# Moving one VectorE addition two units later in the q and k products of an attention kernel

## The chip, the cores and the metric

The kernel runs on one core of one Trainium2 chip. The core has a matrix engine (TensorE, PE in the profile, whose weight loads have a row of their own, PEld), a vector engine (VectorE, DVE), an activation engine (ScalarE, ACT), GpSimd (POOL) and a sync engine that issues DMAs (SyncE, SP). Matmul results land in PSUM[...], and VectorE and ScalarE read them from there.

The metric is the device time of one execution in microseconds (us). The kernel before takes 2177.04 us, the median of three runs from 2176.34 to 2177.31. A difference of less than about 0.2%, some 4.4 us, can't be told from no change.

## What is computed

The input is 8 images of 512 channels and 32 x 32 positions in float32, so each is a 512 x 1024 matrix. Two layers follow each other:

```python
# layer 0: attention with 8 heads of 64 channels
q = conv1x1(x, Wq, bq);  k = conv1x1(x, Wk, bk);  v = conv1x1(x, Wv, bv)
attn = softmax(einsum('bhdn,bhdm->bhnm', q, k) * scale)
x = x + conv1x1(einsum('bhnm,bhdm->bhdn', attn, v), Wp, bp)
# layer 1: a non-local block without softmax, then a batch norm
f = einsum('bcn,bdn->bcd', theta(x), phi(x)) / n
z = conv1x1(einsum('bcd,bdn->bcn', f, g(x)), W_w, W_b) + x
out = (z - mean(z)) * rsqrt(var(z) + eps) * gamma + beta
```

The change concerns `q` and `k` alone. Each is a product of a 512 x 512 weight and a 512 x 1024 image, plus a bias for each channel.

## The kernel before, in words

**Order of the stages.** The loop at the end of `unshifted` goes through the images. For image b it runs the attention, then q of image b+1, v of image b+1, k of image b+1, then the projection (`pp`) of image b with Wp, then theta and phi (`ptp`), and then the non-local block. TensorE's instructions have a fixed order (`pe` keeps them in program order), so these stages lie behind each other on TensorE.

**A product by seven.** The large products are done in the manner of Winograd's variant of Strassen's scheme, by `seven`: weight and data are cut into quarters 11, 12, 21 and 22, and seven products of quarters, or of sums of quarters, are added to the four quarters of the result. `SEVEN` (line 220) lists for each product its name, the weight and the data that it takes, the PSUM slot and the quarters that read the slot. A slot[...] holds one quarter product of 256 x 512. Some products are added up in the slot itself and read again in between.

**q and k.** From the second image on, three of the seven quarter products are cut in the same way once more (`nested`, line 240): 3 times 7 inner products of 128 x 256, each with an add into q or k on VectorE, or a first write on ScalarE. The other four are full quarter products (`FOUR`, line 234): product 0 is W11 x11, product 1 is s1t1, product 2 is s2t2, product 3 is s3t3. Products 0, 2 and 3 add up in slot 0, and product 1 alone lies in slot 1. The full products are spread over 16 units (`HALVES`), each unit being one 128 x 128 x 512 matmul of the code; float32 shows each of them as two rows in the trace. Product 1 is done by units 4, 5, 10 and 11. After each unit come so many inner products as `STEPS` says: two after each of units 5 to 12, one after units 13, 14 and 15. The inner products are counted here from 0 to 20; 14 and 15 follow unit 11, 16 and 17 follow unit 12, 18 follows unit 13, 19 unit 14 and 20 unit 15.

**Inner products wait for adds.** In one inner round, products 0, 2, 4 and 6 share a place in PSUM, and 1 and 3 share another. So inner product 16 can't start before VectorE has added inner product 14 to q or k, 17 waits for the add of 15, 18 for that of 16, and 20 for that of 18.

**Reading the slots.** `READS` (lines 237 and 238) says after which unit a slot of the full products is read, and for which quarter. A read marked `True` is the first for its quarter and is done by ScalarE as two activations of 128 x 512 with the bias (line 386). One marked `False` is an add on VectorE of 128 x 1024 (line 319). Within a unit these reads stand ahead of the unit's inner products, except in unit 15.

**Order on VectorE.** In q the adds have a fixed order (`pin` is `dve`, which keeps them in program order). In k they have none of their own: a planner that lays out the instructions of each engine in advance may put them elsewhere. VectorE also makes differences of image data in these stages (`more_sums`, line 201, and `inner_parts`, line 213): the dictionary `fills` puts them behind a unit, in k after units 5, 7, 11, 12, 13 and 14.

**PSUM tags.** When a stage ends, its slots go to the next. Slot 0 of the stage that follows (v after q, `pp` after k) is slot 1 of q or k.

Of the kernel before, what the change touches and what calls it, by code (L numbers as in the profile page):

```python
# [22 lines left out]
def attention_nonlocal_kernel(tc: tile.TileContext, a: dict, out: bass.AP):  # L23

    sound = unshifted(tc, a, out)
    with tc.If(sound < P):
        shifted(tc, a, out)
# [3 lines left out]
def unshifted(ctx: ExitStack, tc: tile.TileContext, a: dict, out: bass.AP):  # L31
# [184 lines left out]
    def quarters_of(t):  # L216
# [17 lines left out]
    FOUR = tuple((*one[:4], ()) for one in (SEVEN[0], SEVEN[1], SEVEN[2], FIVE[4]))  # L234
    HALVES = ((0, 0), (0, 1), (1, 0), (2, 0), (2, 1), (1, 1), (3, 0), (3, 1))
    STEPS = {2: [0] * 4 + [1] * 14, 3: [0, 0, 0, 1, 1, 2, 2, 2, 2, 2, 2, 2, 2, 1, 1, 1]}
    READS = {3: ((0, "11", True),), 9: ((0, "12", True),), 11: ((1, "22", True), (1, "12", False)),
             15: ((0, "22", False), (0, "21", False))}

    def nested(name, stage, w, data, tags, first, add):  # L240
# [17 lines left out]
    def seven(name, w, data, positions_out, first, add, between=None, early=False,  # L258
# [14 lines left out]
        def read(reads, ps):  # L273
            for to, is_first in reads:
                (first if is_first else add)(to, ps)

        products = FOUR if three else FIVE if inner else EARLY if early else SEVEN
        for n, m in HALVES if three else ((n, None) for n in range(len(products))):
# [15 lines left out]
            for to_ps, at, lhsT, rhs, k in work:  # L294
# [3 lines left out]
                for ahead in (True, False):  # L298
                    for one, to, is_first in READS.get(unit, ()) if three and ahead == (unit < 15) else ():
                        read(((to, is_first),), slots[one])  # L300
# [818 lines left out]
```

## Time and profile before

| what | value | how to read it |
|---|---|---|
| time | 2177.04 us | median of three runs |
| span of the profiled run | 2174.1 us | first to last instruction |
| TensorE busy | 2129.2 us (98%) | matmuls are pipelined, so this is not TensorE at its peak |
| VectorE busy | 1399.6 us (64%) | an average over stages of very different load |
| ScalarE busy | 746.5 us (34%) | |
| granted TensorE clock | 0.996 | nearly full speed throughout |
| DMA | 106 GB/s mean | |
| `q<-q,pq_in_s`, 128 x 256 | 119 x 419 ns | adds of inner products on VectorE |
| `q<-q,pq`, 128 x 1024 | 25 x 1216 ns | adds of full products on VectorE |
| `q<-pq,bq`, 128 x 512 | 48 x 684 ns | first writes on ScalarE |

In a timeline each row gives start and duration in us, engine, line, operation, output and inputs, the shape, how often it came in a row, and in brackets how long the engine had been idle before it and what released it. In a list of waits the columns are the total in us, how often, and the longest.

### The profile page before, as it was taken

The numbers are of one execution on the slowest core, as the hardware profiler recorded it, in microseconds if no ns is written. First come the engines' busy times: TensorE is split into PE (matmuls) and PEld (weight loads), VectorE is DVE, ScalarE is ACT, GpSimd is POOL, SyncE is SP. The second block draws the span as 40 slices with busy tenths as digits, with TensorE's granted clock in tenths as the row PEclk, the third lists the DMA queues.
The fourth block names the chain that finished last, engine by engine and source line by source line (L and its number), as shares of the span: only waits on it lengthen the run. The fifth ranks groups of instructions, "written<-read, shape, count | busy, mean of one in ns | idle before, by whom it ended". The sixth has DMA issues, their size and how long they took to land.

```text
span 2174.1 us, 30056 instructions
## 1 busy us (share of the span) xinstructions
PE 2129.2 (98%) x12510; PEld 1120.5 (52%) x12510; DVE 1399.6 (64%) x1690; ACT 746.5 (34%) x854; POOL 205.1 (9%) x256
## 2 busy tenths in 40 slices
PE   9999999999999999999999999999999999999996
PEld 4534664356733567335663366633666337643462
DVE  6466756666576665766657666576674675757736
ACT  1464104631046310463105621056212652056206
POOL 0111100110001100011000100011000110011000
PEclk9999999999999999999999999999999999999998
DMA  6333443334143331433324342233434235122658
GB/s 219 136 49 61 136 154 124 49 69 128 72 129 50 77 115 72 132 50 77 111 87 119 49 94 92 105 105 49 106 122 166 40 47 137 51 56 39 216 204 337
DMA packets 53375, 229.97 MB, mean 106 GB/s; under 512 B 9712, under 2 KB 16112, under 8 KB 45680
## 3 DMA queue, kind: packets, MB, share of 16 engines
q1 hardware_dynamic: 41552, 198.21, 27.0%
q0 software_dynamic: 10192, 28.46, 10.9%
q8 instruction: 100, 1.64, 0.3%
q10 hardware_dynamic: 1488, 1.32, 0.2%
q14 instruction: 43, 0.35, 0.0%
HBM read 140.79 MB, written 46.27 MB: 86 GB/s over the span
## 4 chain that ended last, share of the span: by engine, by line
PE 94%; ACT 2%; DVE 2%; DMA 1%; issue 0%; ACTq 0%; DVEq 0%
PE ps L456 20%; PE po L482 20%; PE pv L295 9%; PE ptp L295 9%; PE pp L295 7%; PE pk L295 5%; PE pq L295 5%; PE pg L295 4%; PE pq_in_s L250 3%; PE pk_in_s L250 3%; PE pf L622 3%; PE pz L295 2%; PE pp_in_s L250 2%; PE pwf L657 1%; ACT z L773 1%; DVE k L319 1%
## 5 line engine op out<-in xcount | busy, mean ns | idle before, releaser
L459 ACT ACTIVATE e<-ps 128x1024 f32<-128x1024 f32 x512 | 522.9, 1025 | 433.5 <-PE ps L456 428.0
L465 DVE TENSOR_TENSOR acc<-acc,e 128x1024 f32<-128x1024 f32 x384 | 470.0, 1224 | 144.6 <-ACT e L459 141.3
L482 PE MATMUL po<-e,v 64*64 64x512 f32 x4096 | 528.7, 589 | 0.7 <-ACT w_WgT L624 0.7
L456 PE MATMUL ps<-q,k 64*64 64x512 f32 x4096 | 529.1, 589 | 0.0
L482 PEld LDWEIGHTS po<-e,v 64*64 64x64 f32 x4096 | 156.5, 133 | 283.4 <-issue 275.7
L456 PEld LDWEIGHTS ps<-q,k 64*64 64x64 f32 x4096 | 155.6, 133 | 284.1 <-issue 275.0
L495 POOL DMA_DIRECT2D fold<-acc x189 | 147.2, 779 | 984.9 <-DMA fold<-acc 583.4
L463 DVE TENSOR_TENSOR acc<-e,e 128x1024 f32<-128x1024 f32 x64 | 78.3, 1224 | 143.7 <-ACT e L459 143.7
L645 ACT ACTIVATE g<-pg,gb 128x512 f32<-128x512 f32 x31 | 21.3, 687 | 418.9 <-PE pg L295 418.8
L295 PE MATMUL pv<-w_WvT,t_x 128*128 128x256 f32 x512 | 116.4, 381 | 0.0
L295 PE MATMUL ptp<-w_tp,t_x 128*128 128x256 f32 x512 | 114.4, 379 | 0.0
L411 ACT COPY v<-pv 128x1024 f32<-128x1024 f32 x32 | 32.4, 1012 | 224.6 <-PE pv L295 224.6
L295 PEld LDWEIGHTS pv<-w_WvT,t_x 128*128 128x128 f32 x512 | 96.6, 190 | 18.5 <-issue 5.7
L295 PEld LDWEIGHTS ptp<-w_tp,t_x 128*128 128x128 f32 x512 | 97.3, 190 | 13.2
L423 POOL TENSOR_SCALAR q<-q,gates 128x1024 f32<-128x1024 f32 x32 | 35.3, 1114 | 700.3 <-DVE gates L421 700.3
L295 PE MATMUL pp<-t_o,w_WpT 128*128 128x512 f32 x208 | 100.8, 592 | 0.0
L295 PE MATMUL pq<-t_x,w_WqT 128*128 128x512 f32 x200 | 99.9, 593 | 0.4 <-DVE w_WqT L784 0.4
L295 PE MATMUL pk<-t_x,w_WkT 128*128 128x512 f32 x200 | 100.0, 592 | 0.0
L295 PE MATMUL ptp<-w_tp,x 128*128 128x256 f32 x384 | 87.4, 381 | 0.0
L295 PE MATMUL pv<-w_WvT,x 128*128 128x256 f32 x384 | 86.8, 379 | 0.0
L319 DVE TENSOR_TENSOR q<-q,pq_in_s 128x256 f32<-128x256 f32 x119 | 48.3, 419 | 49.1 <-PE pq_in_s L250 46.0
L295 PEld LDWEIGHTS ptp<-w_tp,x 128*128 128x128 f32 x384 | 72.4, 190 | 13.0 <-issue 3.6
(179 smaller groups left out, 2282.9 us busy)
## 6 DMA issues: line engine op xcount, KB each, us to landing
fold<-acc POOLq DMA_DIRECT2D x189, 128.0 KB, 3.1
w_WqT<-kept_WqT SPq DMA_DIRECT2D x7, 2368.0 KB, 8.9
w_WkT<-kept_WkT SPq DMA_DIRECT2D x7, 2368.0 KB, 9.0
r<-den_d SPq DMA_DIRECT2D x32, 512.0 KB, 7.1
x<-in_x_dram SPq DMA_DIRECT2D x31, 512.0 KB, 6.0
w_WpT<-kept_WpT SPq DMA_DIRECT2D x6, 2176.0 KB, 8.6
w_WvT<-kept_WvT SPq DMA_DIRECT2D x7, 1792.0 KB, 7.1
w_tp<-kept_tp SPq DMA_DIRECT2D x7, 1792.0 KB, 7.3
```

The lines of the kernel that those rows point to most:

```text
L250: pe(nc.tensor.matmul(ps, a[wi], d[di], start=s not in begun, stop=True, skip_group_check=True))
L295: pe(nc.tensor.matmul(to_ps, lhsT(k), rhs(k), start=(s, at) not in begun, stop=(k == nk - 1), skip_group_check=True))
L319: pin(nc.vector.tensor_tensor(at, at, ps if len(ps.shape) == 3 else ps.unsqueeze(1), ALU.add))
L411: seven(f"pv_{b}", w, data, True, lambda q, ps: nc.scalar.copy(at(q), as_v(ps)), lambda q, ps: dve(nc.vector.tensor_tensor(at(q), at(q), a ...
L423: nc.gpsimd.tensor_scalar(q[:, p, :], q[:, p, :], gate[:, p:p + 1], 1.0, ALU.mult, ALU.mult)
L456: pe(nc.tensor.matmul(ps[c * P // 2:(c + 1) * P // 2, j, :], k[r, p, keys], q[r, p, h * 512:(h + 1) * 512], start=True, stop=True, skip_gr ...
L459: nc.scalar.activation(e, ps, AF.Exp, scale=SCALE)
L463: nc.vector.tensor_tensor(accs[u], es[u, 0], e, ALU.add)
L465: ins = nc.vector.tensor_tensor(accs[u], accs[u], e, ALU.add)
L482: pe(nc.tensor.matmul(ps[j * D:(j + 1) * D, r, :], v[keys, m, (2 * p + j) * D:(2 * p + j + 1) * D], e[keys, j, :], start=(m == 0), stop=(m ...
L495: nc.gpsimd.dma_start(to, part_of, accum_op=ALU.add)
L622: pe(nc.tensor.matmul(ps[:, c, :], tp[:, i, c * P:(c + 1) * P], tp[:, i, CI:], start=(i == 0), stop=(i == NB - 1)))
```

## The change

The addition of product 1 (slot 1) to quarter 12 moves from unit 11 to unit 13. At unit 11 there stays only ScalarE's first write of quarter 22 from the same slot. The instruction itself is the same, and no other is added or removed. It is meant to keep VectorE free for the adds of the inner products while ScalarE reads slot 1, so that the addition stands in VectorE's queue where the slot is free to be read.

```diff
-    READS = {3: ((0, "11", True),), 9: ((0, "12", True),), 11: ((1, "22", True), (1, "12", False)),
+    READS = {3: ((0, "11", True),), 9: ((0, "12", True),), 11: ((1, "22", True),), 13: ((1, "12", False),),
              15: ((0, "22", False), (0, "21", False))}
```

`READS` is used by the stages with three inner rounds only: q and k of images 1 to 7, 14 stages in all.

## The prediction

> **What bounds the kernel now.** I read the page first, then TensorE's waits, then the timeline of one q stage and one k stage. The share of the chain that ended last says whose time counts:
>
> ```profile
> PE 94%; ACT 2%; DVE 2%; DMA 1%; issue 0%; ACTq 0%; DVEq 0%
> ```
>
> TensorE carries the span, so only time taken from TensorE's row counts. The little that isn't PE in this chain is where the change can act. TensorE's waits, longest first, show where:
>
> ```profile
> PE pk_in_s L250 <- DVE k L319: 10.1, 8, 1.4
> PE pq_in_s L250 <- DVE q L319: 9.9, 7, 1.4
> PE warm_ps L339 <- DVE heads L325: 1.1, 1, 1.1
> ```
>
> Of all idle time of TensorE, 20.0 us lies in the q and k stages, and it is one wait of 1.42 us in each of the 14 (plus one of 0.23 in the first k). Every one sits in the same place. The timeline of the q stage of image 2, PE's weight loads left out:
>
> ```profile
> 474.36 1.02 PE L295 MATMUL pq<-t_x,w_WqT 128*128 128x512 f32 x2
> 475.22 0.59 PE L250 MATMUL pq_in_s<-x,w_WqT 128*128 128x256 f32 x2
> 475.42 1.27 ACT L386 ACTIVATE q<-pq,bq 128x512 f32<-128x512 f32 x2 [0.38 <-PE pq L295]
> 475.65 0.59 PE L250 MATMUL pq_in_s<-i_x,w_WqT 128*128 128x256 f32 x2
> 476.08 1.02 PE L295 MATMUL pq<-t_x,w_WqT 128*128 128x512 f32 x2
> 476.72 1.22 DVE L319 TENSOR_TENSOR q<-q,pq 128x1024 f32<-128x1024 f32 x1 [2.17 <-ACT q L386]
> ...
> 478.04 0.75 DVE L319 TENSOR_TENSOR q<-q,pq_in_s 128x256 f32<-128x256 f32 x2
> ...
> 478.52 0.70 PE L250 MATMUL pq_in_s<-i_x,w_WqT 128*128 128x256 f32 x2 [1.42 <-DVE q L319]
> 479.06 0.59 PE L250 MATMUL pq_in_s<-x,w_WqT 128*128 128x256 f32 x2
> ```
>
> The first row is unit 11. ScalarE reads slot 1 for quarter 22 from 475.42 to 476.69. The add to quarter 12 reads the same slot: VectorE stands idle for 2.17 us, released by that ScalarE read, and starts at 476.72. Behind it in VectorE's queue are the adds of inner products 14 and 15 (478.04, the second 0.33 later). Inner product 16 waits for the first and begins at 478.52.
>
> How much is lost? I take the cadence rather than the 1.42 us, since matmul ends are modelled. A unit takes 0.86 us (474.36 to 475.22), an inner product 0.43 (475.22 to 475.65). With unit 12 at 476.08, product 16 is due at 476.94, product 17 at 477.37 and unit 13 at 477.80. In the trace unit 13 comes at 479.49: **1.69 us lost** a q stage. The waits of product 17 hide in the shorter idle figure.
>
> [...] the add starts 0.03 us after ScalarE ends. [...] the adds of products 14 and 15 stay behind an add that does nothing for 2.17 us.[...]
>
> **The change in q** (order on VectorE fixed). Nothing is added, and the 1.22 us add is only moved. An inner add starts 0.63 us after its matmul (product 12: 473.50, add 474.13). So:
> - Add 14 runs 475.85 to 476.27, add 15 476.28 to 476.70. Products 16 and 17, due at 476.94 and 477.37, no longer wait, and unit 13 comes at 477.80.
> - Add 16 runs 477.57 to 477.99, add 17 478.00 to 478.42. The moved add follows. Its wait for ScalarE is over since 476.69 and its data are there since unit 11, so it runs from about 478.5 to 479.7.
> - Queued behind it: add 18, which would start at 479.29 (product 18 at 478.66) and now starts 1.32 us after the moved add (as 478.04 follows 476.72), about 479.85, and ends at 480.27. Who waits for it is product 20, due at 481.24: 0.97 us to spare.
> - The next stage's first matmul, in v, takes over slot 1 at 481.67 instead of 483.36. The moved add has left it at 479.7, 2 us before.
>
> I therefore count the full 1.69 us: 7 x 1.69 = **11.8 us**. If the moved add were slower to start by a whole unit, the 0.97 us would still cover it.
>
> **The change in k.** Here VectorE also makes data differences, and its queue is full:
>
> ```profile
> 526.58 1.22 DVE L319 TENSOR_TENSOR k<-k,pk 128x1024 f32<-128x1024 f32 x1 [2.17 <-ACT k L386]
> 527.91 0.75 DVE L319 TENSOR_TENSOR k<-k,pk_in_s 128x256 f32<-128x256 f32 x2
> 528.57 1.22 DVE L201 TENSOR_TENSOR t_o<-o 128x1024 f32<-128x1024 f32 x1
> 529.71 0.94 DVE L319 TENSOR_TENSOR k<-k,pk_in_s 128x256 f32<-128x256 f32 x2
> 530.57 1.22 DVE L201 TENSOR_TENSOR t_o<-o,t_o 128x1024 f32<-128x1024 f32 x1
> 531.71 0.41 DVE L319 TENSOR_TENSOR k<-k,pk_in_s 128x256 f32<-128x256 f32 x1
> ```
>
> From 526.58 on no row has idle time before it until `pp` runs. Unit 12 is at 525.94 and `pp` begins at 533.30, 7.36 us later. Without waits there are 4 units and 5 inner products: 4 x 0.86 + 5 x 0.43 = 5.59, so **1.77 us** is lost here. In the new order, with the spacings of these rows (0.33 after an inner add, 1.14 after a difference): add 14 at 525.71, 15 at 526.14, difference 526.47, add 16 at 527.61, 17 at 527.94, difference 528.27, moved add 529.41, add 18 at 530.73, ending at 531.15. Product 20 is due at 531.10 and starts some 0.05 after its add, so it waits 0.1: 1.67 us gained in a stage.
>
> VectorE's queue of this stage now begins 0.87 us earlier (525.71 for 526.58), while TensorE is 1.67 earlier. So VectorE enters `pp` about 0.8 later against TensorE; of that 0.3 falls into an idle 0.21 to 0.30 that stands there now. The tightest place in `pp`: inner product 2 there starts at 540.17, and its slot is read by an add from 539.26 to 539.68, 0.44 to spare. I get a wait of about 0.2 for the six k stages followed by a `pp` with inner products. The first k stage has a plain `pp` instead, which already waits 0.43 for VectorE; only VectorE's earlier start of 0.9 to 1.3 counts, and I take 1.1. Sum for k: 6 x (1.67 - 0.2) + 1.1 = **9.9 us**.
>
> **What hides nothing.** The other stages run on TensorE with no wait over 0.7 us, apart from 1.1 at the very start. The two DMA-fed steps after q have room: the last transfer of the softmax sums is issued at 478.10, and with its 3.1 us of landing is there by 482, while the matmul that reads it begins at 490.36. The granted clock is 0.996, so there is no throttle to give the time back.
>
> Sum: 11.8 + 9.9 = 21.7; 2177.04 - 21.7 = **2155.3 us**.
>
> **Rivals.**
> - *Forecast, both stages gain* (0.80): from 7 x 1.69 + 7 x 1.77 = 24.2 us, nothing lost again, 2152.8, to 2159 if each `pp` loses 0.8 instead of 0.2.
> - *k gives it back* (0.13). For it speaks that k's adds have no fixed order, and that VectorE there is full: inner adds and differences already lie crosswise (a difference of `i_o` at 532.04 stands between adds 18 and 19). If the planner puts the moved add behind the four `i_o` differences, it runs 531.5 to 532.7, and `pp`, whose first slot it reads, starts near 532.75 instead of 533.30: 0.55 us a stage, 7 x 0.55 - 1.2 = 2.7 for k, **2162.5**; with nothing left for k 2165.2. Against it: in the k stage before, the add stands at its place in the program, in spite of its wait.
> - *The wait only moves* (0.04): product 20 waits for add 18 as long as product 16 did, **2177**. Against it speaks the 0.97 us to spare in q.
> - *Slower* (0.03): k's moved add goes last, behind the two closing adds of 2.35 us. It would end near 535.0, and `pp` would start at 535.1, 1.8 later than now: 7 x 1.8 = 12.6; with no gain in q **2189.6**. Nothing in the profile shows q or k laid out so.
>
> **Numbers.** The range takes in all of the forecast's bounds and the gentler part of the second case: 2152.0 to 2161.0. Faster by over 0.2% (below 2172.7) are the first two cases, 0.93; the same 0.04; slower 0.03.
>
> **What would show it.** In the q stage: no idle time before product 16, the 128x1024 add behind four inner adds with no release by ACT, unit 13 1.72 us after unit 12. TensorE's waits for DVE in q gone; in k at most some 0.1. In `pp_in_s` a new wait for DVE of some 0.2, six times. The prediction is wrong if product 18 or 20, or the first `pv` or `pp` matmul, shows a wait over 0.5 us.

## The result, and the profile after

The changed kernel takes **2154.97 us** (median of four runs, 2154.47 to 2155.29) against 2176.93 for the kernel before on the same chip (2176.34 to 2177.31). The ratio is 0.9899 with a 95% interval of 0.9882 to 0.9916: 22.0 us faster.

TensorE's list of waits after the change, in full (total in us, times, longest):

```profile
PE warm_ps L339 <- DVE heads L325: 1.1, 1, 1.1
PE pq L295 <- DVE w_WqT L784: 1.0, 1, 1.0
PE pk_in_s L250 <- DVE k L319: 0.7, 2, 0.5
PE po L482 <- ACT w_WgT L624: 0.7, 1, 0.7
PE den L428 <- PE pg L295: 0.5, 1, 0.5
PE pp L295 <- DVE k L319: 0.3, 1, 0.3
```

The row of q is gone. That of k is down from 10.1 to 0.7 us, and what is left of it lies in the first k stage. The same stretch of the q stage of image 2, weight loads left out:

```profile
471.77 1.02 PE L295 MATMUL pq<-t_x,w_WqT 128*128 128x512 f32 x2
...
472.83 1.26 ACT L386 ACTIVATE q<-pq,bq 128x512 f32<-128x512 f32 x2 [0.39 <-PE pq L295]
...
473.33 0.78 DVE L319 TENSOR_TENSOR q<-q,pq_in_s 128x256 f32<-128x256 f32 x2 [1.37 <-PE pq_in_s L250]
473.49 1.02 PE L295 MATMUL pq<-t_x,w_WqT 128*128 128x512 f32 x2
474.35 0.59 PE L250 MATMUL pq_in_s<-i_x,w_WqT 128*128 128x256 f32 x2
...
474.98 0.94 DVE L319 TENSOR_TENSOR q<-q,pq_in_s 128x256 f32<-128x256 f32 x2 [0.87 <-PE pq_in_s L250]
475.21 1.02 PE L295 MATMUL pq<-t_x,w_WqT 128*128 128x512 f32 x2
...
476.03 1.22 DVE L319 TENSOR_TENSOR q<-q,pq 128x1024 f32<-128x1024 f32 x1
```

Unit 11 is at 471.77, unit 12 at 473.49, unit 13 at 475.21: 1.72 us each time, where the kernel before took 3.41 from unit 12 to 13. While ScalarE reads slot 1 (472.83 to 474.09), VectorE does the adds of inner products 14 and 15. (ScalarE writes to q in that time, and so do these adds, so it isn't q itself that keeps the two engines apart. What is left for them to share is slot 1.) The moved add at 476.03 has no idle time before it, and nothing from ScalarE releases it. From unit 12 to the first matmul of v, at 479.08, it is 5.59 us.

In the k stage that follows, VectorE's queue is still without a gap behind add 15, and TensorE waits once, for 0.3 us, ahead of inner product 20:

```profile
523.35 0.94 DVE L319 TENSOR_TENSOR k<-k,pk_in_s 128x256 f32<-128x256 f32 x2
524.20 1.22 DVE L201 TENSOR_TENSOR t_o<-o,t_o 128x1024 f32<-128x1024 f32 x1
525.33 1.21 DVE L319 TENSOR_TENSOR k<-k,pk 128x1024 f32<-128x1024 f32 x1
525.97 1.02 PE L295 MATMUL pk<-t_x,w_WkT 128*128 128x512 f32 x2
526.65 0.42 DVE L319 TENSOR_TENSOR k<-k,pk_in_s 128x256 f32<-128x256 f32 x1
527.13 0.70 PE L250 MATMUL pk_in_s<-i_x,w_WkT 128*128 128x256 f32 x2
527.66 3.60 PE L295 MATMUL pp<-o,w_WpT 128*128 128x512 f32 x8
```

Unit 15 is at 525.97, so product 20 is due at 526.83. Its row comes at 527.13, just behind add 18, which ends at 527.07. The list of waits doesn't have this wait. It shows only in the distance between the rows, and in a longer row (0.70 for 0.59). From unit 12 (521.67) to `pp` it is 5.99 us, where 7.36 were before and 5.59 are the least.

Where the time came from can be read stage by stage, from the start of each stage on TensorE in the two traces. Each q stage is 1.7 us shorter (12.2 in all, with one of 2.0), the first k 0.9, and the six other k stages 1.36 each (8.1). Together that is 21.2 us, and the profiled spans differ by 21.1 (2174.1 and 2153.0). No other stage changed by more than 0.3. Two of these figures hold scatter. Of the 2.0 in one q stage, 0.35 is a delay in the trace of the kernel before, which the kernel with q left alone (below) lacks too. And the first k, 0.9 shorter here, is 1.7 shorter in a second profile of the same changed kernel.

### The profile page after: what moved, and what is told of

It is laid out like the page before. It is cut to its first block, busy times and chain, and to the rows that moved or that the text cites. A ratio compares the mean times of both kernels' runs of the same rounds, so it can differ in the third digit from the quotient of the medians.

```text
span 2153.0 us, 30084 instructions
## 1 busy us (share of the span) xinstructions
PE 2126.0 (99%) x12510; PEld 1121.3 (52%) x12510; DVE 1399.4 (65%) x1690; ACT 746.1 (35%) x854; POOL 204.9 (10%) x256
## 4 chain that ended last, share of the span: by engine, by line
PE 94%; DVE 3%; ACT 2%; DMA 1%; issue 1%; DVEq 0%; SPq 0%; ACTq 0%
PE ps L456 20%; PE po L482 20%; PE pv L295 9%; PE ptp L295 9%; PE pp L295 7%; PE pq L295 5%; PE pk L295 4%; PE pg L295 4%; PE pq_in_s L250 3%; PE pf L622 3%; PE pz L295 2%; PE pk_in_s L250 2%; PE pp_in_s L250 2%; DVE k L319 1%; ACT z L773 1%; PE pwf L657 1%
## 5 line engine op out<-in xcount | busy, mean ns | idle before, releaser
L319 DVE TENSOR_TENSOR k<-k,pk_in_s 128x256 f32<-128x256 f32 x119 | 48.3, 419 | 55.6 <-PE pk_in_s L250 41.9
## 6 DMA issues: line engine op xcount, KB each, us to landing
w_WpT<-kept_WpT SPq DMA_DIRECT2D x6, 2176.0 KB, 8.5
```

Of the source, the lines that this page charges most:

```text
L319: pin(nc.vector.tensor_tensor(at, at, ps if len(ps.shape) == 3 else ps.unsqueeze(1), ALU.add))
```

## The experiments

Theory A is the prediction's: VectorE's queue stood behind an add that waited for ScalarE on the same slot. Theory B: the wait is a side effect, and what costs is a 1.22 us add ahead of the inner adds.

**The other way round.** The add stays at unit 11, ahead of ScalarE's read:

```diff
-    11: ((1, "22", True), (1, "12", False))
+    11: ((1, "12", False), (1, "22", True))
```

> The moved add stays at unit 11, but ahead of ScalarE's read of slot 1: VectorE reads the slot first, ScalarE waits. The instructions of every engine and their order are those of the kernel before; only the direction of one wait differs. Theory A (VectorE's queue stands behind an add that waits for ScalarE on the same slot): VectorE starts the add about 1.2 us earlier, right after unit 11; add 14 then ends about 0.1 to 0.2 after product 16 is due, so most of the 1.69 us of each stage comes back: 2154 to 2158 us. Theory B (the wait is a side effect; what costs is that a 1.22 us add lies ahead of adds 14 and 15 in the queue): that order is unchanged, so 2172 to 2178 us.

Measured: 2159.61 us against 2176.28, ratio 0.9924 (0.9907 to 0.994). The queues of all engines hold the same instructions in the same order as before the change. The q stage of image 2:

```profile
472.89 1.22 DVE L319 TENSOR_TENSOR q<-q,pq 128x1024 f32<-128x1024 f32 x1 [0.94 <-PE pq L295]
...
474.15 1.26 ACT L386 ACTIVATE q<-pq,bq 128x512 f32<-128x512 f32 x2 [1.71 <-DVE q L319]
474.22 0.75 DVE L319 TENSOR_TENSOR q<-q,pq_in_s 128x256 f32<-128x256 f32 x2
474.70 0.70 PE L250 MATMUL pq_in_s<-i_x,w_WqT 128*128 128x256 f32 x2 [0.19 <-DVE q L319]
```

Now ScalarE is the one that waits (1.71 us, released by VectorE), and TensorE waits for nothing of ScalarE's here. TensorE's wait falls from 1.42 to 0.19. So the direction of one wait is worth 16.7 us of the 22, and theory B, with its order unchanged, falls. It keeps a share: 1.23 us a stage came back, not 1.69 (in q). The 0.46 that stay lost fit the add's own length ahead of adds 14 and 15: add 14 ends at about 474.6, 0.3 after product 16 is due. I had put that at 0.1 to 0.2, and the time lies 1.6 us above my range.

**ScalarE's read twice over, before and after.** The same edit in both kernels makes ScalarE's reading longer and leaves the values alone:

```diff
-    (1, "22", True)
+    (1, "22", True), (1, "22", True)
```

> The kernel before, with ScalarE's two activations of slot 1 for quarter 22 done twice over (the same values written again), 1.26 us more of ScalarE reading at unit 11. Theory A: the add starts 1.26 later, and TensorE's wait in each of the 14 stages grows by as much, 14 x 1.26 = 17.7: 2194.7 us. Theory B: ScalarE is 34% busy and the wait a side effect, so 2177 us.

> The changed kernel, with ScalarE's read of slot 1 for quarter 22 done twice over. Theory A: in q ScalarE leaves the slot at about 474.1 + 0.0 instead of 472.8 + 1.3, some 2 us before the moved add's turn at 476.0, so nothing waits: 2155 us (within 1). If the position at unit 13 does not in fact lie behind ScalarE's reading, part of 17.7 us shows up.

Measured: the kernel before goes to 2198.68 us (2195.24 to 2200.57) from 2176.28, ratio 1.0106 (1.0089 to 1.0122). The changed kernel stays at 2154.1 against 2176.0, ratio 0.9899 (0.9883 to 0.9916). (In the changed kernel with the double read, ScalarE reads from 472.46 to 474.88 in the q stage of image 2, and the moved add starts at 475.66, still 0.78 us behind it. The expectation had some 2 us, which is the distance with the single read.) The kernel before, in the q stage of image 3:

```profile
752.82 1.22 DVE L319 TENSOR_TENSOR q<-q,pq 128x1024 f32<-128x1024 f32 x1 [3.32 <-ACT q L386]
...
754.61 0.70 PE L250 MATMUL pq_in_s<-i_x,w_WqT 128*128 128x256 f32 x2 [2.57 <-DVE q L319]
```

VectorE's idle time grows from 2.17 to 3.32 and TensorE's from 1.42 to 2.57, both by 1.15, which is what ScalarE's four activations take longer than two (2.42 us, not 1.27; the expectation had taken 1.26 more). The same extra reading costs the changed kernel nothing. That settles what was waited for.

14 x 1.15 is 16.1, but 22.4 us were lost by the medians and 19.4 between the profiled runs. The 3.3 us that the profiled run lost beyond the 16.1 are a matter of the clock, told in the last section.

**One stage alone.** The add moves in q only, or in k only; the other keeps it at unit 11.

```diff
-    ... READS.get(unit, ()) ...
+    ... (READS if inner == "WqT" else AT_11).get(unit, ()) ...   # "WkT" for k alone
```

> The add moves to unit 13 in q alone; k keeps it at unit 11. Theory A: the stages gain apart from each other, 7 x 1.69 = 11.8 us, so 2165.1 us, with TensorE's wait of 1.42 us in each k and none in q. Rival (the gain in one stage is handed on and lost or doubled in the next, through slots, transfers or VectorE's backlog): more than 2 us away from that.

> The add moves to unit 13 in k alone; q keeps it at unit 11. From the starts of the stages in the two traces k gains 6 x 1.36 + 0.9 = 9.1 us: 2167.8 us under theory A. Under the rival that k's gain is only had together with q's, 2172 or more.

Measured: 2164.53 for q alone (ratio 0.9946, 0.9929 to 0.9962) and 2166.49 for k alone (0.9956, 0.9939 to 0.9972), against 2176.28. That is 11.75 and 9.79 us, 21.5 together, for 22.0 with both. The gains add up. With q alone the six later k stages, and with k alone six of the seven q stages, are as long as in the kernel before to within 0.02 us. The seventh is the one with the delay of 0.35 named above. The first k is 0.5 longer with q alone, less than the 0.8 by which two profiles of the changed kernel differ there. The rival in which k gives it back falls.

**Other places.** The add goes to unit 12, 14 or 15 (the first two lines for units 12 and 14; for unit 15 the line of unit 13 goes, and the last two lines hold):

```diff
-    13: ((1, "12", False),),
+    12: ((1, "12", False),),                # or 14
-    15: ((0, "22", False), (0, "21", False))
+    15: ((1, "12", False), (0, "22", False), (0, "21", False))
```

> The add moves by one unit only, to unit 12, ahead of adds 16 and 17 and behind 14 and 15. Theory A with VectorE's queue written out: q loses nothing (add 16 ends about 478.5 in the old trace's times, product 18 is due at 478.66), so q keeps its 1.69. In k the difference of unit 11 lies in front, so add 16 ends 0.9 after product 18 is due: k loses 0.9 instead of the 0.4 of the changed kernel, 7 x 0.5 = 3.5 us: 2158.4 us. Rival (any place behind adds 14 and 15 is as good as another): 2155.0 us.

> The add moves to unit 14. Theory A: q loses nothing (add 18 goes first; the slot is left at 481.1 in the old trace's times, 0.6 before the next stage's first matmul). In k product 20 no longer waits, but the slot is left later, and the first matmul of pp, which takes it over, waits about 0.4 instead: 2155 us, 2153.5 to 2156.5. Rival (later is always better): 2152 us.

> The add moves to unit 15, behind the add of inner product 20. Theory A: the next stage's first matmul takes over slot 1 and now waits for this add: in q it ends about 483.5 in the old trace's times, 1.9 after v is due, in k about as late, so nothing is gained: 2177 to 2181 us. Rival (the slot's next user does not matter): 2155 us.

| place of the add | time, us | before in the same runs | ratio, 95% interval |
|---|---|---|---|
| unit 12 | 2158.77 | 2176.0 | 0.992 (0.9904 to 0.9937) |
| unit 13 (the change) | 2154.97 | 2176.93 | 0.9899 (0.9882 to 0.9916) |
| unit 14 | 2152.97 | 2176.0 | 0.9894 (0.9877 to 0.991) |
| unit 15 | 2196.06 | 2176.0 | 1.0095 (1.0078 to 1.0112) |

Unit 13 differs from units 12 and 14 by less than the 4.4 us that can be told by time alone. What tells them apart are the stages, which in a trace repeat within 0.02 us (the first k aside). Unit 12 came nearly as worked out: q 0.05 us a stage longer than at unit 13, k 0.59 longer. Unit 14 came out 0.5 us below its range: product 20 no longer waits (k 0.39 shorter), and `pp` starts with its slot just left by the moved add. In the k stage of image 2:

```profile
525.89 1.22 DVE L319 TENSOR_TENSOR k<-k,pk 128x1024 f32<-128x1024 f32 x1
526.72 0.59 PE L250 MATMUL pk_in_s<-i_x,w_WkT 128*128 128x256 f32 x2
527.02 0.42 DVE L213 TENSOR_TENSOR i_o<-o,i_o 128x256 f32<-128x256 f32 x1
527.16 3.27 PE L295 MATMUL pp<-o,w_WpT 128*128 128x512 f32 x7
```

The add ends at 527.11. The wait of 0.4 that I expected there does not come, since the planner put the add behind one difference only. Instead `pp` itself is 0.15 longer.

At unit 15 the add runs into the next user of its slot, as expected, but it costs far more. The k stage of image 3 there:

```profile
806.29 3.47 DVE L319 TENSOR_TENSOR k<-k,pk 128x1024 f32<-128x1024 f32 x3
808.74 2.05 PE L295 MATMUL pp<-o,w_WpT 128*128 128x512 f32 x2 [2.82 <-issue]
```

The planner put the moved add among the two closing adds, three in a row, and `pp` starts behind the second of them. TensorE stands idle for 2.82 us, where some 1.9 were expected, and in v for 1.84, as expected. The row calls the releaser "issue", but it begins just as the second add ends (806.29 plus two adds of 1.2). Which of the three is the moved one the rows don't tell; that it is the second is my reading. Against the changed kernel, stage by stage, q is 2.0 us longer (14.0 in all), as expected, but k is 18.7 longer, where 7 x 1.9 would be some 13, and three `pp` stages lose another 5.8, on which the last section has the clock. So the window is three units wide: from unit 12, where the queue has let adds 14 and 15 pass, to unit 14, where the slot is still left in time.

**The residue in k.** VectorE is idle for 1.37 us ahead of add 14 and overloaded behind it. Two data differences move into that gap:

```diff
-    ((5, 1), (7, 2), (11, 3), (12, 4))
+    ((5, 1), (7, 2), (10, 3), (11, 4))
```

> The changed kernel itself, for comparison on the same chip: 2154 to 2155.3 us.

> The changed kernel, with the third and fourth difference of o in k moved one unit earlier each (units 10 and 11 instead of 11 and 12), where VectorE stands idle for 1.37 us before add 14. If what is left of k's loss (0.40 us a stage, product 20 waiting for add 18) is VectorE's backlog behind the two differences, add 18 now ends 0.8 before product 20 is due and pp is not late either: 6 x 0.40 = 2.4 us less than the changed kernel, 2152 to 2152.7 us. If the residue is something else (the time of TensorE's own rows), 2154 to 2155.

> As sums_earlier, with the add at unit 14. Under the same reasoning neither product 20 nor the first inner products of pp wait in either place, so the two differ by less than 1 us: 2151.5 to 2153 us.

Measured: the changed kernel 2154.12, the differences earlier **2151.59** (ratio to before 0.9887, 0.9871 to 0.9904), the same with the add at unit 14 2152.2 (0.9891, 0.9874 to 0.9907); before 2176.13. In the k stage of image 2, with the differences earlier:

```profile
524.88 0.42 DVE L319 TENSOR_TENSOR k<-k,pk_in_s 128x256 f32<-128x256 f32 x1
525.14 1.02 PE L295 MATMUL pk<-t_x,w_WkT 128*128 128x512 f32 x2
...
526.00 0.59 PE L250 MATMUL pk_in_s<-i_x,w_WkT 128*128 128x256 f32 x2
```

Add 18 ends at 525.30, 0.7 before product 20 is due, and product 20 comes 0.86 after unit 15. Each of the six stages is 0.40 shorter than in the changed kernel, all that was lost there. By the medians this version beats both kernels, but 2.5 us is less than can be told by time alone, and the intervals of the two ratios overlap. What carries it is the traces, in which all six stages show the same 0.40.

## Why the prediction was right, point by point

- **The bound.** That TensorE's waits in q and k are real time holds: they are gone, and the span is shorter by nearly what the cadence said they cost, but for 0.40 us in each of six k stages.
- **The size.** Taking 1.69 us from the cadence, not the 1.42 of the idle column, was right for q: 7 times 1.42 would have been 9.9. Forecast for q 11.8, measured 11.8 (alone, from the times) and 12.2 (between the traces, 0.35 of it the late stage of the kernel before).
- **The mechanism.** The two reads of slot 1 follow each other in either order: in the kernel before the add starts 0.03 us after ScalarE's read ends, and in the swapped kernel ScalarE starts 0.04 us after VectorE's add ends. That they could not overlap, no run here shows. The adds of products 14 and 15 stay behind the waiting add in the doubled read too: in q of image 3 VectorE is idle for 3.32 us, up to 752.82, though both products are done by 752.05, when TensorE falls idle.
- **VectorE's order in q.** As written out: adds 14, 15, 16, 17, the moved add, add 18. I had the moved add at 478.5, unit 12 plus 2.4; it stands at unit 12 plus 2.54. Product 20 did not wait.
- **k.** Forecast 6 x (1.67 - 0.2) + 1.1 = 9.9; measured 6 x 1.36 + 0.9 = 9.1. Two terms were off, in opposite directions, so that the sum for k comes as near as it does is in part luck. The wait of product 20 was to be 0.1; it is 0.30, and the product itself then takes 0.53 instead of 0.43, so 0.40 is lost. I spaced adds 16 and 17 by 0.33 us, but their pair takes 0.94, so the second starts 0.52 after the first. The prediction's own lines had it: the same pair takes 0.94 at 529.71. In `SEVEN` both go to the same quarter (`s2t2` and `s4` to 12), and the chain that ended last has, between them, a step of VectorE's sequencer (DVEq) that waits for the first:

```profile
523.43 0.34 DVE k L319
...
523.79 0.02 DVEq L319
...
523.86 0.42 DVE k L319
```

 The wait of 0.2 in `pp` did not come. It does not follow from its own figures either: 0.8 less the 0.3 of idle time and the 0.44 to spare leaves 0.06, or 0.15 with the 0.21 of the idle row. With the change, add and product in the tightest place lie 0.20 apart (533.92 + 0.42 to 534.54), since `pp` starts later by what k lost. At unit 14, where k loses next to nothing, `pp` is 0.15 longer, so a backlog of that size fits, though VectorE's order differs there.
- **The first k** gained 0.9 for 1.1 in the first profile and 1.7 in the second, so this term lies within its scatter.
- **A misreading without effect.** The 3.1 us of landing for the last transfer of the softmax sums belongs to another group. The one issued at 478.10 (`fold<-fold` on POOL) has a median of 4.7 us, which leaves it landed by 483, still far ahead of 490.36.
- **The chain that ended last.** In the kernel before it leads in q from ScalarE's read (475.42) through the waiting add (476.72) and add 14 (478.04) to product 16, just as the prediction has it. With the change it stays on TensorE in q. VectorE's share still went up a little, since in the k stage of image 2 the chain now leads through VectorE's full queue, from add 14 to add 18:

```profile
PE 94%; DVE 3%; ACT 2%; DMA 1%; issue 1%; DVEq 0%; SPq 0%; ACTq 0%
```

- **The rivals.** That k gives it back is refuted by the k-only kernel. That the wait only moves, by the timeline of q. That an add placed last makes the kernel slower is true of unit 15 (2196.06 us). The prediction's 2189.6 was for the change itself with k's add behind the closing adds, which did not happen.

## What to carry to other kernels

When an engine waits on a shared buffer, look at what is queued behind it, not at the waiting instruction: here an add whose result no one needed soon held up two that TensorE needed at once (VectorE idle for 2.17 us, TensorE for 1.42). The add has a window here, units 12 to 14: it begins when the other reader has left the slot and the urgent work has passed, and ends where the slot's next user is due. Count a repeated wait by the distance between steady instructions rather than by the idle column, and look for idle time just ahead of the overload: moving other work into it brought back the last 0.40 us of each of the six k stages.

## What the runs showed of the hardware

After some of TensorE's waits the granted clock was 0.50. After the 14 waits of 1.42 us of the kernel before it was not: in the 3 us behind each it was 1.00. In the kernel before with ScalarE's read doubled, q stages with the same wait of 2.57 us differ. The rows below give a stretch of time, its length, the busy time of TensorE and the other engines, and, third from the end, the granted clock. The wait of image 2 (480.96 to 483.53) lies in the first row almost whole, that of image 3 (752.05 to 754.61) only in part in the third. The second and the fourth row are the stretches behind them:

```profile
480.07:483.48 3.41, 0.89 (x3) 0.06 (x1) 1.65 (x3) 1.63 (x3) 0.86 (x1) 1.00 0.15 13
483.48:486.89 3.41, 3.36 (x6) 2.19 (x7) 1.17 (x3) 0.00 (x0) 0.00 (x0) 0.50 0.49 64
753.13:756.54 3.41, 1.93 (x7) 1.34 (x8) 2.50 (x5) 0.00 (x0) 0.86 (x1) 1.00 0.43 40
756.55:759.96 3.41, 3.41 (x14) 2.25 (x13) 1.15 (x3) 0.00 (x0) 0.00 (x0) 1.00 0.21 36
```

In image 2 the clock was 0.50 for 3.41 us, and this stage lost 2.80 us against the kernel before, where image 3 lost 1.15. So one such drop costs some 1.65 us, near half of 3.41, and two of the 14 stages of the profiled run had it. That different numbers of drops make the spread of 5.3 us between runs of this kernel is an estimate, about three drops of 1.65 us; the mean granted clock was 0.995 in the profiled run, of 2195.24 us, and 0.992 in the longest, of 2200.57. Only one of the four was profiled. With the add at unit 15 a clock of 0.50 is seen in three `pp` stages, after two of the six waits of 2.82 us and after one of 3.63 ahead of the first. Here in the same way a wait of 2.82 us (805.92 to 808.74) with a drop behind it, and another (1615.57 to 1618.40) without one:

```profile
805.16:808.57 3.41, 0.76 (x3) 0.19 (x1) 3.41 (x7) 0.00 (x0) 0.00 (x0) 1.00 0.52 135
808.58:811.98 3.40, 3.24 (x4) 1.51 (x5) 2.62 (x6) 0.00 (x0) 0.00 (x0) 0.50 0.94 401
1614.12:1617.53 3.41, 1.45 (x5) 0.57 (x3) 3.38 (x8) 0.00 (x0) 0.00 (x0) 1.00 0.39 71
1617.54:1620.94 3.40, 2.54 (x6) 1.25 (x7) 3.31 (x6) 0.00 (x0) 0.00 (x0) 1.00 0.93 396
```

The length of a wait alone does not decide it: of two waits of 2.57 us, and of two of 2.82, one has a drop behind it and the other has none. In the rows above, TensorE was busy for 0.89 and 0.76 us of the 3.41 ahead of the two drops, and for 1.93 and 1.45 in the rows ahead of the two at 1.00. What decides between them was not shown. In the q stage of image 2 a wait 1.8 times as long (2.57 us for 1.42) lost 2.7 times as much: 1.69 + 2.80 = 4.49 us, for 1.69.
